# A hybrid attention kernel: the fill of the causal layer moved behind the value products, with a rate for each key tile, and V's staging tile chosen by layer

## The chip, the cores and the metric

One core of one Trainium2 chip runs the kernel; the other seven are idle. The metric is the device time of one execution in microseconds (us). The engines are PE (TensorE: matmuls into PSUM banks), PEld (its weight loads), DVE (VectorE), ACT (ScalarE), POOL (GpSimd) and SP (SyncE, which here only issues DMAs). Each works through its own queue in order, and they wait for each other by semaphores.

## The reference

Sixteen sequences of 512 tokens and 256 channels pass through four attention layers, each with 16 heads of 16 channels: a causal one ("a"), one with two token groups ("f"), a rotary one ("b"), and "f" again with the same weights.

```python
x = x + attn_a(layernorm(x))     # causal
x = x + ffn(layernorm(x))        # attention within two groups of tokens
x = x + attn_b(layernorm(x))     # rotary
x = x + ffn(layernorm(x))

def attn_a(x):
    Q, K, V = x @ Wq.T + bq, x @ Wk.T + bk, x @ Wv.T + bv
    ...
    scores = einsum('bhqd,bhkd->bhqk', Qh, Kh) / sqrt(16)
    scores = where(idxs[None, :] <= idxs[:, None], scores, -10000.0)
    out = einsum('bhqk,bhkd->bqhd', softmax(scores), Vh)
    return out.reshape(b, seq, 256) @ Wo.T + bo

def ffn(x):
    q, k, v = split(x @ W_qkv)
    sim = (cosine of each head of q with a fixed direction).mean(-1)
    pos = (sim - sim.min()) / (sim.max() - sim.min()) > 0.9
    # tokens of pos attend to each other and 5 register tokens, the others likewise
    ...
    return out @ W_proj + b_proj
```

The minimum and maximum of `sim` run over all tokens of all sequences, so an "f" layer's attention can only begin when every sequence has been prepared for it.

## The kernel before

The attention runs over quads: four heads of one sequence in one layer, 4 quads a sequence, 64 a layer. The causal layer is layer 0, with quads 0 to 63. A sequence is called an image in what follows.

**Score products.** For every quad PE makes the scores twice. `maxima` makes them with queries as rows (L610, tile s); DVE takes each row's maximum (in the causal layer with L626, which adds the mask on the way and writes mx after a short read of its accumulator). The maxima go through a small DMA (L654, L657) into additional rows of Q, so that the second product (`products.score`, L687, tile t, keys as rows) comes with the maximum already taken away. In the causal layer two mask products follow each of them (L698). ACT takes the exponential of t into a tile e (L702), and `weigh` multiplies e by V (L713, tile po, four heads side by side, eight matmuls as each is done in two passes), summing over the key tiles. After the last key tile ACT copies po away (L729).

**Key tiles.** A quad has NT = 4 key tiles t of 128 keys, and each has two passes p (two heads each, e = 0, 1). In the causal layer the products of key tile t need only the queries from 128 t on: t is 512, 384, 256 and 128 wide for t = 0, 1, 2, 3. I call t = 0 and 1 wide and t = 2 and 3 narrow. In a narrow tile the two passes share the halves of the same two PSUM tiles. The maxima run AHEAD = 20 steps before the products, so that beside the products of t = 0, 1, 2, 3 stand maxima of 384, 512, 128 and 256 columns. All tiles of PE but po come from one pool, `ps_x`, of seven banks.

**Order.** PE's order is that in which the program issues its work (`manual_schedule` for PE); the order of the other engines is made by a scheduler. For each quad and key tile the main loop (L1108 on) issues a step of the maxima, the score for p = 0, the fill, another step of the maxima, the score for p = 1, and then the value products of the key tile before (`waiting`).

**Fill.** All other work comes as generators in the list `fill`, in order of rank: the preparation of an image for a layer (`prep`: layer norm, transposes L340, V products L467, Q and K products L360, and for "f" the similarity L410 to L434), the share of the masked keys (`masked`, L852 to L856), the tail of an image (`tail`: division, turning back L903, projection L922), and the turning of the maxima (L649). Every generator yields a delay or a condition, and the planned ns of its next step: 1362 for a Q or K product, 1380 for a V product or a projection of two tiles, 450 for transposes, 1750 for the similarity. A planner's clock (`clock["now"]`) decides when a delay is over; it also plans three banks for the fill.

`fill_in` adds RATE[layer] to a credit (2100 ns for layer 0), keeps at most twice that, and calls `drain`, which takes the first step that is able until there is none, or until a step costs more than twice the credit left. Besides, `drain(until=...)` makes fill without credit where something is needed now: before the third quad of an image the image before must be divided, and a quad's Q and K must be prepared before they are loaded.

In layer 0 the fill holds the preparation of image b + 2 for layer 0, that of an earlier image for layer 1, `masked`, and the tail of image b - 1. At the end of the layer all that is left is drained, and `split` makes the groups of layer 1.

**Buffers that matter.** Q and K parts are written into tiles of tag `parts` from pool p4 (two buffers): ACT writes the high part (L398 with bias in layer 0, L401 for "f"), DVE the rest (L399, L402), for Q of "f" GpSimd does both (L380, L381). `send` then issues four DMAs on SP for each (L370, L374) to DRAM, from where `load_quad` (L577, on POOL's queue) fetches whole quads, four ahead. A parts buffer is free when its four DMAs have landed. V is put together in one of two staging tiles `vst`, by b % 2 (L478 by DVE in layer 0, L480 by ACT for the others), and stored by L482 on SP; `load_values` (L583) fetches it back.

Of the kernel before, what the change touches and what calls it, by code (L numbers as in the profile page):

```python
# [119 lines left out]
def hybrid_kernel(ctx: ExitStack, tc: tile.TileContext, a: dict, out: bass.AP):  # L120
# [24 lines left out]
    def small(name, dtype=F32):  # L145
        return ps_x.tile([P, S], dtype, tag="x", name=name)
# [84 lines left out]
    vst = []  # L231
    for i in range(2):
        t = res.tile([P, NT, VW], F32, tag=f"vst{i}", name=f"vst{i}")
# [3 lines left out]
    for i in range(2):  # L237
        t = res.tile([P, RW], FR, tag=f"rst{i}", name=f"rst{i}")
# [61 lines left out]
    def prep(layer, b, x):  # L300
# [154 lines left out]

        def values(u):

            v = vst[b % 2]
            xh, xl = st["xh"], st["xl"]
            ps = small(f"pv{n}_{u}")  # L460
            for k in range(2):
                t = 2 * u + k
                ts = slice(t * P, (t + 1) * P)
                seq = [(xl, wh), (xh, wl), (xh, wh)]
                for q, (xx, ww) in enumerate(seq):
                    for c in range(2):
                        nc.tensor.matmul(  # L467
                            ps[:, k * C : (k + 1) * C],
                            xx[:, c, ts],
                            ww[:, c, WV, :],  # L470
                            start=(q == 0 and c == 0),
                            stop=(q == 2 and c == 1),
                        )
            vo = v[:, 2 * u : 2 * u + 2, 0 : H * HV].rearrange("p t (h e) -> p t h e", e=HV)[:, :, :, 0:D]
            vi = ps.rearrange("p (t h d) -> p t h d", t=2, d=D)
            if kind == "a":
                bias = bv.rearrange("p (h d) -> p h d", d=D).unsqueeze(1).to_broadcast([P, 2, H, D])
                nc.vector.tensor_tensor(vo, vi, bias, ALU.add)  # L478
            else:
                nc.scalar.copy(vo, vi)  # L480
            if u == 1:
                nc.sync.dma_start(vd[b], v)  # L482
# [18 lines left out]
        for u in range(2):  # L501
            yield lag, 1380
            values(u)
            lag = 0
# [69 lines left out]
    def load_quad(i):  # L574
        layer, b, g = quads[i]
        for t, d in ((Qs[i % NB], qd[b]), (Ks[i % NB], kd[b])):
            nc.gpsimd.dma_start(t, d[:, :, 2 * g : 2 * g + 2, :].rearrange("e r h s -> (e r) h s"))  # L577
# [3 lines left out]
    def load_values(layer, b):  # L581
        t = p2.tile([P, NT, VW], F32, tag="v", name=f"v{layer}_{b}")
        nc.sync.dma_start(t, vd[b])  # L583
        V[layer, b] = t
# [406 lines left out]
    def push(gen, rank):  # L991

        k = sum(s.rank <= rank for s in fill)
        fill.insert(k, Steps(gen, rank))

    def push_tail(layer, b):
        push(tail(layer, b), 1)

    def push_call(f, after=None):
        def gen():  # L1000
            yield (lambda: busy["prep"] == 0 and (not after or after in tailed)), 0
            f()

        push(gen(), 1)

    def drain(credit=None, until=None):

        while fill and not (until and until()):
            now = clock["now"]
            able = [s for s in fill if s.ready <= now and (s.next == 0 or banks[0] <= now) and s.open()]  # L1010
            if not able:
                if credit is not None:
                    return
                clock["now"] = min(max(s.ready, banks[0] if s.next else 0) for s in fill if s.open())
                continue
            s = able[0]
            if credit is not None:
                if s.next > 2 * max(0, credit["ns"]):
                    return
                credit["ns"] -= s.next  # L1020
            s.run()

    RATE = {0: 2100, 1: 1350, 2: 1250, 3: 700}
    credit = {"ns": 0}

    def fill_in(layer):

        credit["ns"] = min(credit["ns"] + RATE[layer], 2 * RATE[layer])
        drain(credit)

    def load_through(i):
        while loaded["n"] <= min(i, len(quads) - 1):
            j = loaded["n"]
            layer, b, g = quads[j]
            if (layer, b) not in prepared:
                drain(until=lambda: (layer, b) in prepared)
            if j >= NB:
                l_, b_, g_ = quads[j - NB]
                if PLAN[l_] == "f":
                    drain(until=lambda: (l_, b_, g_ // 2) in registered)  # L1040
            load_quad(j)
            loaded["n"] += 1

    def prep0(b, x=None):
        push(prep(0, b, load_x(0, b) if x is None else x), 2)
        busy["first"] += 1
        constant_rows(b)
# [8 lines left out]
    def advance(to, budget=0):  # L1056

        while taken["n"] < to:
            n = taken["n"]
            load_through(n // (2 * NT))  # L1060
            k, r = divmod(n, 2 * NT)
            if r == 0:
                taken["steps"], taken["end"] = maxima(k)
            taken["steps"][r]()
            clock["now"] += 230
            taken["n"] += 1
            if r == 2 * NT - 1:
                push(taken["end"](), 0)
            if budget:
                at = clock["now"]  # L1070
                drain({"ns": budget})
                clock["now"] = max(clock["now"], at + budget)

    waiting = None
    for i, (layer, b, g) in enumerate(quads):
        kind = PLAN[layer]
        alone = b == 0 and g == 0 and (layer == 0 or kind == "f")
        held = kind != "f" and layer + 1 < len(PLAN) and PLAN[layer + 1] == "f"
        end = (layer + 1) * B * NG if held else len(quads)
        if b or g or layer:  # L1080
            load_through(min(end - 1, i + 4))
        if g == 0:
            load_values(layer, b)
            if kind == "f":
                first, second = registers(layer, b)
                push(first, 2)
                push(second, 2)
        if layer == 0 and g == (1 if b == 0 else 0):
            if b == 0:
                push_call(late_constants)  # L1090
            if b + 2 < B:
                prep0(b + 2)
        if g == 2 and i > NG:
            before = (layer, b - 1) if b else (layer - 1, B - 1)
            drain(until=lambda: before in divided)
        if kind == "a" and g == 1:
            push(masked(b), 2)
        if b == 0 and g == NG - 1 and layer + 1 < len(PLAN):
            push_call(lambda layer=layer: W.__setitem__(layer + 1, load_weights(layer + 1, False)))
        if b == 0 and g == NG - 2:  # L1100
            push_call(lambda layer=layer: WP.__setitem__(layer, load_weights(layer, True)), layer and (layer - 1, B - 1))
        if alone:
            advance((2 * NT) * i + AHEAD, 900)
        if i not in put:
            drain(until=lambda: i in put)
        score, weigh = products(i)
        for t in range(NT):
            for p in range(2):  # L1108
                advance(min(2 * (NT * i + t) + p + 1 + AHEAD, 2 * NT * end))
                score(t, p)  # L1110
                clock["now"] += 230 + TURN
                if p == 0:
                    fill_in(layer)
                elif waiting:
                    waiting()
                    clock["now"] += 868 + TURN
                    waiting = None
            if t == 0 and g == 0 and (b > 0 or (layer > 0 and kind != "f")):
                push_tail(*((layer, b - 1) if b else (layer - 1, B - 1)))
            if i == 0:  # L1120
                load_through(i + 4) if t == NT - 1 else None
            waiting = lambda weigh=weigh, t=t: weigh(t)
        if kind != "f" and b == B - 1 and g == NG - 1 and layer + 1 < len(PLAN):
            waiting()
            waiting = None
            push_tail(layer, b)
            drain()
            split(layer + 1)
# [46 lines left out]
```

## Time and profile before

| what | us |
|---|---|
| runs, median of 3 | 4260.31 (4257.6 to 4260.97) |
| profiled execution | 4242.52 |
| its span, first to last instruction | 4240.7 |
| PE busy | 3937.4 (93%) |
| DVE busy | 3207.0 (76%) |
| ACT busy | 2631.8 (62%) |
| POOL busy | 1820.8 (43%) |
| last mask product of the causal layer ends | 1270.9 |
| mean granted clock of PE | 0.946 |

A time in the text is from the start of the span unless it is a length. In the profile, `out<-in` names tiles, `L610` is a line of the kernel, and what follows an arrow in brackets is the idle time of that engine and what ended it. PE's matmuls are pipelined and their ends are modelled, so their starts tell more than their lengths. The granted clock is the share of PE's full clock.

### The profile page before, as it was taken

The page shows a single profiled execution, that of the slowest core. Times are in us where ns is not written, and L with a number is a line of the kernel's source. Part 1 is how long each engine was busy: PE and PEld are TensorE (multiplying, and loading weights), DVE is VectorE, ACT ScalarE, POOL GpSimd, SP SyncE. Part 2 cuts the span into 40 slices and gives each one's busy share as a digit, 9 for nine tenths or more (in the row PEclk, how much of TensorE's full clock was granted, in tenths as well). Part 3 has the DMA queues.
Part 4 walks back from the last instruction along what each step waited for, and adds up shares of the span by engine and source line. Part 5 has one row for each costly group of instructions (what it writes and reads, how often), then busy time and mean ns, then how long its engine had stood idle before and what let it go on. Part 6 is the DMA issues. An engine that isn't in the chain of part 4 may idle for free.

```text
span 4240.7 us, 79626 instructions
## 1 busy us (share of the span) xinstructions
PE 3937.4 (93%) x27440; PEld 2051.1 (48%) x27440; DVE 3207.0 (76%) x7488; ACT 2631.8 (62%) x5288; POOL 1820.8 (43%) x2421
## 2 busy tenths in 40 slices
PE   3899999999995999999999999999999599999999
PEld 2565656565553444444444444444444334444444
DVE  4676776667654888888888788888886389999996
ACT  1444454444452777777777667777777267777777
POOL 2124545354543256656665634444444412222221
PEclk6899999899996999999999999999999689999999
DMA  9556566666645345555554645455554623333331
GB/s 300 160 159 187 182 200 181 189 184 190 193 128 167 96 137 170 163 149 165 171 162 152 186 146 169 146 167 168 164 157 126 188 85 114 122 116 114 119 121 51
DMA packets 294722, 661.84 MB, mean 156 GB/s; under 512 B 51624, under 2 KB 90032, under 8 KB 294320
## 3 DMA queue, kind: packets, MB, share of 16 engines
q1 hardware_dynamic: 204080, 384.02, 28.9%
q0 software_dynamic: 90240, 272.73, 21.6%
q8 instruction: 219, 3.59, 0.3%
q14 instruction: 183, 1.50, 0.1%
HBM read 379.46 MB, written 298.06 MB: 160 GB/s over the span
## 4 chain that ended last, share of the span: by engine, by line
PE 72%; DVE 10%; DMA 7%; SPq 3%; ACT 3%; issue 3%; POOL 2%; ACTq 0%; DVEq 0%; POOLq 0%
PE po L713 19%; PE s L610 15%; PE t L687 11%; DVE mx L619 5%; PE pv L467 5%; PE pj L922 4%; PE pq L360 4%; DMA qd<-tq 3%; PE pk L360 3%; PE ot L884 2%; POOL nd L432 2%; DVE sc L626 1%; PE rs L759 1%; PE t L698 1%; SPq L568 1%
## 5 line engine op out<-in xcount | busy, mean ns | idle before, releaser
L702 ACT ACTIVATE e<-t 128x512 f32<-128x512 f32 (+2 forms) x3840 | 2017.6, 588 | 824.2 <-PE t L687 538.6
L619 DVE TENSOR_REDUCE mx<-s 128x1 f32<-128x512 f32 x3072 | 1944.4, 681 | 334.7 <-PE s L610 326.2
L610 PE MATMUL s<-ks,qs 52*128 52x512 f32 (+4 forms) x4096 | 1030.8, 481 | 92.3 <-DMA ks<-kd 78.1
L687 PE MATMUL t<-qs,ks 52*128 52x512 f32 (+4 forms) x4096 | 1000.2, 402 | 103.5 <-ACT e L702 35.5
L713 PE MATMUL po<-e,v 128*32 128x512 f32 (+1 forms) x8192 | 1031.1, 576 | 5.1 <-ACT o L729 3.9
L610 PEld LDWEIGHTS s<-ks,qs 48*128 48x128 f32 (+1 forms) x4096 | 429.9, 191 | 1085.7 <-ACT e L702 310.9
L687 PEld LDWEIGHTS t<-qs,ks 50*128 50x128 f32 (+1 forms) x4096 | 496.8, 191 | 302.3 <-DVE mx L619 102.6
L626 DVE CUSTOM_DVE_ANT_0 sc<-s,mask_s_bf 128x128 bf16<-128x128 f32 (+3 forms) x1024 | 497.7, 486 | 160.5 <-PE s L610 78.6
L577 POOL DMA_DIRECT2D qs<-qd x256 | 153.6, 601 | 811.5 <-PE t L687 530.7
L657 POOL DMA_DIRECT2D qs<-md x512 | 268.5, 529 | 543.7 <-DMA md<-ms 516.2
L432 POOL TENSOR_TENSOR nd<-nd,nhalf 128x16 f32<-128x16 f32 x120 | 346.1, 2902 | 22.5 <-DVE nd L423 22.5
L713 PEld LDWEIGHTS po<-e,v 128*32 128x32 f32 x8192 | 162.6, 109 | 271.9 <-issue 194.3
L309 POOL TENSOR_SCALAR xn<-x,nm,st 128x256 f32<-128x256 f32 x256 | 141.4, 557 | 117.7 <-PE xp L340 111.1
L698 PE MATMUL t<-mask_t_bf 64*128 64x128 bf16 x2048 | 189.4, 234 | 0.0
L380 POOL CAST tq<-yq 128x512 fp32r<-128x512 f32 x80 | 49.1, 613 | 267.9 <-DMA qd<-tq 92.5
L884 PE MATMUL ot<-ident,o 128*128 128x128 f32 x1024 | 148.2, 288 | 16.3 <-DVE tq L399 7.1
L577 POOL DMA_DIRECT2D ks<-kd x256 | 140.1, 548 | 52.1 <-issue 14.5
L729 ACT COPY o<-po 128x512 f32<-128x512 f32 x256 | 153.3, 599 | 7.4 <-PE po L713 7.0
L884 PEld LDWEIGHTS ot<-ident,o 128*128 128x128 f32 x1024 | 117.1, 146 | 47.8 <-DVE mx L619 10.1
L340 PE MATMUL xp<-ident,xn 128*128 128x128 f32 x512 | 89.1, 299 | 46.0 <-POOL xn L309 43.7
L930 DVE TENSOR_TENSOR x<-pj,x 128x512 f32<-128x512 f32 x128 | 87.1, 680 | 55.0 <-PE pj L922 50.5
L347 ACT CAST xh<-xp 128x512 fp32r<-128x512 f32 x128 | 76.0, 595 | 84.1 <-PE xp L340 83.9
(358 smaller groups left out, 4991.6 us busy)
## 6 DMA issues: line engine op xcount, KB each, us to landing
qs<-qd POOLq DMA_DIRECT2D x256, 512.0 KB, 4.5
ks<-kd POOLq DMA_DIRECT2D x256, 512.0 KB, 5.3
qd<-tq SPq DMA_DIRECT2D x256, 256.0 KB
kd<-tk SPq DMA_DIRECT2D x256, 256.0 KB
vd<-vst SPq DMA_DIRECT2D x64, 576.0 KB
v<-vd SPq DMA_DIRECT2D x64, 576.0 KB
qd<-tq SPq DMA_DIRECT2D x256, 128.0 KB
kd<-tk SPq DMA_DIRECT2D x256, 128.0 KB
```

The source lines that it names most:

```text
L360: nc.tensor.matmul(dst, ww[:, c, w, cols], xx[:, c, :], start=(k == 0 and c == 0), stop=(k == 2 and c == 1))
L432: nc.gpsimd.tensor_tensor(nd[:, 0, t], nd[:, 0, t], nhalf[:, t], ALU.pow)
L577: nc.gpsimd.dma_start(t, d[:, :, 2 * g : 2 * g + 2, :].rearrange("e r h s -> (e r) h s"))
L610: nc.tensor.matmul(st["ps"][e][:, (p % m) * end :][:, :end], q[r, p, t * P : (t + 1) * P], k[r, p, :end], start=True, stop=True,)
L619: nc.vector.tensor_reduce(st["mx"][:, e, p, t : t + 1], st["ps"][e], AX.X, ALU.max, negate=True)
L626: nc.vector.tensor_tensor_reduce(w, st["ps"][e][:, (i % m) * end :][:, :end], late["mask_s"][:, S - end :], 1.0, -3.0e38, ALU.add, ALU.max ...
L657: nc.gpsimd.dma_start(q[r : r + 2], d[:, e].rearrange("k j t p -> k j (t p)"))
L687: nc.tensor.matmul(ps[e], k[rows[e], p, t * P : (t + 1) * P], q[rows[e], p, q0:], start=True, stop=(kind != "a"),)
L698: nc.tensor.matmul(ps[e][:, :P], mk[:, 0], mk[:, 1], start=False, stop=(o == 1))
L702: st["exp", t] = nc.scalar.activation(e_[:, : m * w], st["ps"][e][:, : m * w], AF.Exp)
L713: mm = nc.tensor.matmul(st["po"][32 * j : 32 * j + 32, q0:], v[:, t, h * HV : h * HV + 32], E.pop((t, j)), start=(t == 0), stop=(t == NT - 1),
L884: nc.tensor.transpose(ps[:, g * P : (g + 1) * P], O[layer, b, g][:, t * P : (t + 1) * P], ident)
```

## The change

```diff
@@ values
-            v = vst[b % 2]
+            v = vst[layer % 2]
...
-    RATE = {0: 2100, 1: 1350, 2: 1250, 3: 700}
+    RATE = {0: (1400, 1400, 2800, 2800), 1: 4 * (1350,), 2: 4 * (1250,), 3: 4 * (700,)}
     credit = {"ns": 0}

-    def fill_in(layer):
+    def fill_in(layer, t):

-        credit["ns"] = min(credit["ns"] + RATE[layer], 2 * RATE[layer])
+        credit["ns"] = min(credit["ns"], RATE[layer][t]) + RATE[layer][t]
         drain(credit)
...
                 score(t, p)
                 clock["now"] += 230 + TURN
-                if p == 0:
-                    fill_in(layer)
-                elif waiting:
+                if p == 0 and layer:
+                    fill_in(layer, t)
+                if p == 1 and waiting:
                     waiting()
                     clock["now"] += 868 + TURN
                     waiting = None
...
             if i == 0:
                 load_through(i + 4) if t == NT - 1 else None
+            if not layer:
+                fill_in(layer, t)
             waiting = lambda weigh=weigh, t=t: weigh(t)
```

In layer 0 the fill of a key tile is issued after both passes of its scores and after the value products of the key tile before, and no longer between the two passes. The credit of layer 0 now depends on the key tile: 1400 ns at t = 0 and 1, 2800 ns at t = 2 and 3; what is carried over is cut to the rate of the tile it is carried into. In layers 1 to 3 place and rate of the fill stay. The tail of the image before, which is put on the list at the first key tile of a new image, is now listed before that tile's fill. V's staging tile is chosen by the layer: all images of layers 0 and 2 use the one, those of layers 1 and 3 the other.

## The prediction

> **What bounds it now.** The causal layer alone is changed, so I read the page first for where that layer lies.
>
> ```profile
> span 4240.7 us, 79626 instructions
> ...
> PE   3899999999995999999999999999999599999999
> ...
> PEclk6899999899996999999999999999999689999999
> ```
>
> The mask products (L698), which only this layer has, end at 1271 us: slices 1 to 11 of 106 us each. PE is at nine tenths there, yet the granted clock falls in it and hardly at all in the layers behind. Next the windows of the steady part and of two short stretches in it (columns: window, its length, busy time and count of PE, weight loads, DVE, ACT, POOL, then granted clock, DMA share, GB/s):
>
> ```profile
> 150.00:1230.00 1080.00, 1012.94 (x8284) 642.74 (x8281) 740.20 (x2750) 519.11 (x1095) 489.41 (x583) 0.93 0.60 181
> ...
> 782.00:788.00 6.00, 5.50 (x37) 3.47 (x38) 3.57 (x15) 2.93 (x7) 6.00 (x3) 0.50 0.56 138
> ```
>
> PE idles 1080 - 1013 = 67 us, and the clock is granted at either full or half (782 to 788 us), so 0.93 means 2 x 0.07 x 1080 = 151 us at half clock. A fit over the 59 quads of this stretch (duration against counts of each kind of fill matmul, idle time and half-clock time, 0.4 us left over) gives 1.06 us for a us of idle and 0.34 us for a us of half clock. So stalls cost 67 + 51 = 118 us here, and the rest is PE work that the change leaves as it is: a quad takes 18.4 us on average. Then who stops PE, and who stops ACT (us in total, times, longest):
>
> ```profile
> PE t L687 <- ACT e L702: 24.9, 12, 5.7
> PE t L687 <- DVE tk L402: 7.2, 5, 1.9
> PE ot L884 <- DVE tq L399: 7.1, 4, 2.2
> ...
> PE t L687 <- DVE mx L626: 3.8, 8, 1.7
> PE t L687 <- DVE tk L399: 2.4, 2, 1.4
> ```
> ```profile
> ACT tk L401 <- DMA qd<-tq: 44.7, 13, 7.0
> ACT tk L398 <- DMA qd<-tq: 35.0, 18, 5.1
> ```
>
> The score products wait for exponentials, and ACT stands before a copy of K or Q into one of two send buffers (pool p4), whose last DMA has not landed; DVE's half of the copy stands with it. One such case in the timeline (start, length; PE, then ACT):
>
> ```profile
> 549.55 0.62 PE L360 MATMUL pk<-xh,whq 128*128 128x512 f32 x2
> ...
> 553.05 0.85 PE L713 MATMUL po<-e,v 128*32 128x384 f32 x8
> 553.83 0.39 PE L610 MATMUL s<-ks,qs 48*128 48x256 f32 x2
> 554.07 0.32 PE L687 MATMUL t<-qs,ks 50*128 50x128 f32 x1
> 558.52 0.47 PE L687 MATMUL t<-qs,ks 50*128 50x128 f32 x1 [4.13 <-ACT e L702]
> ```
> ```profile
> 557.39 0.59 ACT L401 CAST tk<-pk 128x512 fp32r<-128x512 f32 x1 [5.51 <-DMA qd<-tq]
> 557.87 1.09 ACT L702 ACTIVATE e<-t 128x512 f32<-128x512 f32 x2
> ```
>
> ACT stands from 551.9 to 557.4; PE goes on until all seven PSUM banks of ps_x are held, and stops at the second tile of t=3, whose exponentials come behind the copy. Last, ACT and DVE in the wide and the narrow tiles, by shape (busy us, mean ns, idle):
>
> ```profile
> L702 ACT ACTIVATE e<-t 128x512 f32<-128x512 f32 x354 | 192.2, 596 | 145.3 <-PE t L698 144.5
> L626 DVE CUSTOM_DVE_ANT_0 sc<-s,mask_s_bf 128x512 bf16<-128x512 f32 x232 | 159.3, 687 | 33.6 <-PE s L610 14.2
> L626 DVE DVE_READ_ACCUMULATOR2_ANT mx<- 128x1 f32 x939 | 77.6, 83 | 0.0
> ```
>
> **The change, part by part.** It adds and removes no instruction of the tensor work. I write F(t) for the fill in the round of key tile t.
>
> *The place of the fill.* Before, a round is [t, F, s, t, po]; after, [s, t, s, t, po, F]. What counts is how much PE can do once a copy in F has stopped ACT and DVE: it ends when seven banks are held, one by the copy's own product. For t=2 and 3 both pairs of heads share a tile (two banks for s, two for t). Before, F stands inside them: four banks held, one for the copy, two for the next s, and PE has left s, t, masks, po and the next s. With spacings from the timeline (two s 0.17 to 0.43 us by width, two t 0.17 to 0.45, four masks 0.2, eight po 0.21 to 0.85) that is 1.3 us for F(2) and F(3), 1.9 for F(1), 1.6 for F(0). After, F(1) and F(2) are followed by a whole narrow round in four banks, its po, and two steps of the next fill of 1.42 us each (pk, 548.52 to 549.9): 4.3 to 4.5 us. F(3) and F(0) are followed by a wide round in which s, t, s take six banks: 1.3 to 1.4 us. So the half of the fill that stands in F(1) and F(2) gains some 2.8 us of cover, the other half loses 0.2. The order on ACT and DVE isn't written out, so the copies may stand elsewhere in it; hence both ends.
>
> The waits that this bears on are 24.9 + 7.2 + 2.4 = 34.5 us. None gone gives 0; all gone gives -34.5, and with their part of the half clock, 34.5/67 x 51 = 26, -60. I take half of both, as half of the fill is covered: -17 and -13, **-30 us**.
>
> *How far the clock follows.* Half-clock spells begin behind waits as short as 1.2 to 2.2 us in this trace (2.15 us at 653 us, half clock from 655.7), so I let the clock follow the idle time. The Trainium skill, "TensorE: Matmul & The Clock Gate", section "HAM oscillation — how this bites in real kernels", has as its abstract rule that only gaps of more than about 3.4 us matter. By it, only the four waits over 3.4 us would count, the clock's share of the gain would mostly fall away, and the sum would be some -9 instead of -22. The trace's short waits speak against it here.
>
> *The wide rounds.* In a round of t=0 or 1 eight tiles come with no fill and no po between, so the last t needs the first s reduced: 0.55 to 0.69 us plus 0.08 for the read, behind DVE's copy of the fill's last product (0.75). Before, po (0.21 or 0.85 us) stood among these eight. Nothing in the trace shows this order. Lower end: 0, if DVE keeps up. Upper end: the whole po time missed in both wide rounds and a little less, 0.8 us a quad x 64 = +51. Nearest is today's row for it, t waiting for mx, 3.8 us in 59 quads; with less room I take three times that, **+8 us** more.
>
> *The rates.* A quad's credit stays 4 x 2100 = 1400 + 1400 + 2800 + 2800 = 8400 ns. With steps of 1362 the pattern goes from 2, 1, 2, 1 to 1, 1, 2, 2. A wide round with one step is level on three engines: t=0 has 4 x 0.596 + 0.595 for o + 0.69 for a copy = 3.7 us on ACT, 3.6 on PE (2.13 + 1.42); t=1 has 4 x 0.77 + 0.75 = 3.8 on DVE, 4.2 on PE. PE leads or is level everywhere, so I cost this at **0**; without a step in a wide round the cover is gone, and ACT's 2.98 or DVE's 3.08 stand against 2.13 or 2.77 of PE: 0.3 to 0.85 us lost in each. Unused credit carried into a wide round is now cut to 1400 (2100 before), so late fill catches up more slowly; today one forced drain each 12 quads (quad 17, 29, 41, 53 take 29 to 30 us) costs about 2.2 of idle and 10 us of half clock, 5.6 us: from -22 (all four go) to +56 (ten more), taken as 0.
>
> *V's staging.* One buffer for a layer adds a wait of the V copies (DVE L478, ACT L480) for the last store of the same layer (L482). In the trace such copies lie at least 43 us behind that store's issue, and the page's DMA rows land loads of like size in 4.5 to 5.3 us: **0**. Without that cover the copy would hold DVE's maxima behind it for about 5 us an image.
>
> *Queues.* A fill step's sends (four issues on SP, 0.6 us each) move with it, by less than a round. F(3) now ends a quad, so its GpSimd work (xn 0.56, pow 2.9 us) is ahead of the next load_quad on that queue; the load serves the quad four later, 73 us on. The tail's x load and GpSimd addition come one round earlier. All 0.
>
> **Sum:** -30 + 8 = -22 us. Against the profiled execution (4242.5 us, 1.8 of it around the span) that is 4220; the runs' median, 4260.3, stands 17.8 above it, so **4238 us**.
>
> **The rivals.**
> - *Relief and new waits cancel.* The wide rounds cost 26 rather than 8: -30 + 26, **4256 us**. For it: ACT and DVE have as little room in wide rounds as shown. Against: mx waits are rare today.
> - *Slower: the send buffers.* Two steps in each of F(2) and F(3) put four copies within two rounds, one per 2.2 us instead of 3.1, while a buffer comes free 7 us after its fill (GpSimd finishes a tq at 550.4 in the case above, ACT gets its buffer at 557.4), one per 3.5. The fourth copy is late by 3 x (3.5 - 2.2) = 3.9 us, against 1.2 before: 2.7 more, in F(3), where only 1.3 are covered: 1.4 us in each of 32 preparations, +45, and with a half-clock spell of 7 us (x 0.34) in half of them +38. With -30 - 4: **4309 us**. It decides once copies wait over about 3 us in F(3). For it: ACT's 80 us of such waits. Against: the steps are seldom all ready together.
> - *Fill comes late.* Half of the 128 wide rounds find no step (0.58 us each, +37), and +8: with -30, **4275 us**. For it: the cut credit. Against: the credit is 8400 for about 7340 of planned work.
>
> **How the numbers follow.** Forecast 0.50, cancelling 0.14, send buffers 0.20, late fill 0.16. The forecast's own range is 4190 to 4252. About 0.2% (8.5 us) is what a measurement tells from no change, so faster 0.50, same 0.14, slower 0.36. The range must hold most of the last two: 4180 to 4325; below it lie the whole 60 us and vanished drains, above it both slower mechanisms at once.
>
> **What would show it.** Right: t waiting for e or tk falls from 34.5 to about 17 us in the causal layer, the clock there from 0.93 to about 0.95, its last mask product comes near 1249 us, and the later layers keep their lengths. Wrong: ACT's waits of tk or tq for DMA growing beyond 80 us, t waiting for mx far above 12 us, more quads of 29 us, or a wait at L478 or L480. A change in the layers behind would make the whole argument wrong.

## The result, and the profile after

The changed kernel takes 4305.55 us (median of 4 runs, 4292.49 to 4311.03), the kernel before 4258.95 in the same comparison: 1.0112 times as long, 95% interval 1.0079 to 1.0144. It is slower by 47 us, where a gain of 22 was forecast. The page of the profiled execution (4310.3 us):

```profile
span 4308.3 us, 79671 instructions
...
PE   3898999999995999999999999999999599999999
...
PEclk6789999889897799999999989999999789999999
```

The instructions are the same in number on every computing engine. In slices 1 to 11 of the causal layer (counted from 0, as in the prediction) the clock's digit is under 9 five times, against twice before. The windows from the first to the last mask product, first of the kernel before, then of the changed one (columns as in the prediction):

```profile
100.90:1270.90 1170.00, 1091.06 (x8882) 689.00 (x8882) 777.69 (x2876) 558.36 (x1180) 516.10 (x613) 0.92 0.59 177
```
```profile
99.30:1316.90 1217.60, 1129.24 (x8882) 707.01 (x8885) 792.33 (x2876) 555.37 (x1180) 509.13 (x610) 0.89 0.57 169
```

The layer is 47.6 us longer. PE's idle time in it is 88.4 us against 78.9, and by the clock records 262 us against 180 are at half clock. Another 19 us of the difference between the two spans lie behind `split`, where place and rate of the fill are the old ones (2919 us before, 2938 after); the seven variants below that keep two send buffers and the whole computation take 2922 to 2939 us there, so I count this as spread between executions. The profiled execution of the kernel before is also quicker than most of its executions, 4242.5 us against a median of 4259. What PE waited for in the changed kernel, in the stretch of the prediction (150 to 1230 us):

```profile
PE t L687 <- ACT e L702: 21.2, 15, 3.1
PE t L687 <- DVE mx L626: 12.8, 46, 1.4
PE s L610 <- DVE tk L399: 8.6, 4, 3.8
PE s L610 <- ACT e L702: 7.6, 7, 1.5
PE s L610 <- DVE tk L402: 4.9, 1, 4.9
PE t L687 <- DVE tk L402: 4.3, 1, 4.3
```

PE's waits for exponentials (e) and for copies of K and Q (tk, tq) haven't shrunk, over the whole layer 49 us before and 56 after; a good part has moved from t to s. ACT's copies, in the same stretch:

```profile
ACT tk L398 <- DMA qd<-tq: 54.9, 14, 6.7
ACT tk L401 <- DMA qd<-tq: 23.0, 6, 5.3
ACT tk L401 <- DMA vd<-vst: 17.6, 2, 9.0
ACT tq L398 <- DMA kd<-tk: 5.7, 2, 5.3
ACT tq L398 <- DMA qd<-tq: 4.3, 1, 4.3
```

That is 105 us, against 91 before. One such case in the timeline, PE and then ACT:

```profile
415.71 0.62 PE L360 MATMUL pk<-xh,whq 128*128 128x512 f32 x2
...
417.70 0.66 PE L340 MATMUL xp<-ident,xn 128*128 128x128 f32 x4
...
418.82 0.71 PE L687 MATMUL t<-qs,ks 50*128 50x512 f32 x2
...
424.57 0.69 PE L610 MATMUL s<-ks,qs 48*128 48x384 f32 x1 [4.90 <-DVE tk L402]
```
```profile
423.21 0.58 ACT L401 CAST tk<-pk 128x512 fp32r<-128x512 f32 x1 [5.26 <-DMA qd<-tq]
```

The copy stands in F(2). PE gets through the narrow round behind it and two small steps of F(3) (xp and st), then into the wide round of the next quad, and stops, out of banks, 3.3 us after the product. ACT stands until 423.2 and PE loses 4.9 us.

### The profile page after: what moved, and what is told of

Same layout as the page of the kernel before. It is cut to its first block, busy times and chain, and to the rows that moved or that the text cites. A ratio compares the mean times of both kernels' runs of the same rounds, so it can differ in the third digit from the quotient of the medians.

```text
span 4308.3 us, 79671 instructions
## 1 busy us (share of the span) xinstructions
PE 3988.8 (93%) x27440; PEld 2074.4 (48%) x27440; DVE 3222.0 (75%) x7488; ACT 2628.1 (61%) x5288; POOL 1815.2 (42%) x2421
## 4 chain that ended last, share of the span: by engine, by line
PE 55%; DVE 7%; ACT 2%; SPq 2%; DMA 2%; issue 1%; POOL 1%; ACTq 0%; POOLq 0%; DVEq 0%
PE po L713 16%; PE s L610 12%; PE t L687 9%; DVE mx L619 5%; PE pj L922 3%; PE pv L467 3%; PE pq L360 2%; PE pk L360 2%; PE ot L884 2%; PE rs L759 1%; SPq L568 1%; ACT e L702 1%; PE pa L903 1%; POOL nd L432 1%; PE mt L649 1%
## 5 line engine op out<-in xcount | busy, mean ns | idle before, releaser
L610 PE MATMUL s<-ks,qs 52*128 52x512 f32 (+4 forms) x4096 | 1047.3, 483 | 117.7 <-DMA ks<-kd 81.3
L687 PE MATMUL t<-qs,ks 52*128 52x512 f32 (+4 forms) x4096 | 1023.2, 408 | 109.4 <-ACT e L702 35.8
L713 PE MATMUL po<-e,v 128*32 128x512 f32 (+1 forms) x8192 | 1052.1, 587 | 4.6 <-ACT e L702 3.4
L610 PEld LDWEIGHTS s<-ks,qs 48*128 48x128 f32 (+1 forms) x4096 | 443.7, 194 | 1017.6 <-ACT e L702 300.0
L698 PE MATMUL t<-mask_t_bf 64*128 64x128 bf16 x2048 | 198.6, 237 | 0.0
L402 DVE TENSOR_TENSOR tk<-pk,tk 128x512 fp32r<-128x512 f32 x64 | 44.1, 689 | 132.0 <-ACT tk L401 122.2
```

What stands on the lines that cost most here:

```text
L610: nc.tensor.matmul(st["ps"][e][:, (p % m) * end :][:, :end], q[r, p, t * P : (t + 1) * P], k[r, p, :end], start=True, stop=True,)
L687: nc.tensor.matmul(ps[e], k[rows[e], p, t * P : (t + 1) * P], q[rows[e], p, q0:], start=True, stop=(kind != "a"),)
L698: nc.tensor.matmul(ps[e][:, :P], mk[:, 0], mk[:, 1], start=False, stop=(o == 1))
L713: mm = nc.tensor.matmul(st["po"][32 * j : 32 * j + 32, q0:], v[:, t, h * HV : h * HV + 32], E.pop((t, j)), start=(t == 0), stop=(t == NT - 1),
```

## The experiments

Each was timed in five rounds beside the kernel before on one chip; the ratio is to that kernel. The other columns are in us, for the causal layer, from one profiled execution each: the length from first to last mask product, PE's idle time in it, time at half clock, and the rest, length - 1.06 x idle - 0.38 x half clock (fits over the quads of five of these kernels give 0.86 to 1.08 and 0.33 to 0.42 for the two factors). One execution is a small sample: before and e3_staging issue PE's work of this layer in the same order and are equally fast, and yet differ by 14 us in length and 42 in time at half clock.

| run | what | ratio (95%) | length | idle | half | rest |
|---|---|---|---|---|---|---|
| before | | 1 | 1170 | 79 | 180 | 1018 |
| after | the change | 1.0112 (1.0079 to 1.0144) | 1218 | 88 | 262 | 1024 |
| e1_place | place, even rate | 0.9949 (0.9929 to 0.9969) | 1145 | 66 | 149 | 1018 |
| e2_rates | rates, old place | 1.0072 (1.0052 to 1.0092) | 1208 | 89 | 235 | 1024 |
| e3_staging | staging alone | 0.9997 (0.9978 to 1.0016) | 1184 | 77 | 222 | 1018 |
| e6_wide | place, rates turned round | 1.0144 (1.0124 to 1.0164) | 1227 | 115 | 253 | 1010 |
| e7_cap | change, carry as before | 1.0030 (1.0015 to 1.0046) | 1181 | 76 | 209 | 1021 |
| e16_after_one | change, one copy a fill | 1.0069 (1.0049 to 1.0089) | 1190 | 104 | 189 | 1007 |
| e17_place_one | even rate, one copy a fill | 1.0029 (1.0014 to 1.0044) | 1182 | 88 | 199 | 1014 |
| e5_before_send3 | before, 3 send buffers | 0.9852 (0.9833 to 0.9871) | 1140 | 54 | 160 | 1022 |
| e4_send3 | change, 3 send buffers | 0.9858 (0.9837 to 0.9878) | 1137 | 61 | 141 | 1020 |
| e12_cap_send3 | change, carry, 3 buffers | 0.9856 (0.9833 to 0.9878) | 1140 | 64 | 151 | 1015 |
| e9_place_send3 | even rate, 3 buffers | 0.9753 (0.9735 to 0.9771) | 1092 | 40 | 98 | 1012 |
| e22_before_send4 | before, 4 buffers | 0.9799 (0.9776 to 0.9823) | 1116 | 49 | 123 | 1017 |
| e20_after_send4 | change, 4 buffers | 0.9725 (0.9710 to 0.9740) | 1094 | 44 | 85 | 1016 |
| e21_place_send4 | even rate, 4 buffers | 0.9716 (0.9699 to 0.9733) | 1081 | 36 | 82 | 1012 |
| e13_after_fixed | change, sends from a fixed tile | 1.0048 (1.0031 to 1.0064) | 1245 | 156 | 273 | 975 |
| e15_before_fixed | before, sends from a fixed tile | 1.0090 (1.0074 to 1.0107) | 1255 | 173 | 261 | 973 |

### The parts of the change

```diff
 # e1_place: after, with
-    RATE = {0: (1400, 1400, 2800, 2800), ...
+    RATE = {0: 4 * (2100,), ...
 # e2_rates: after, with
-                if p == 0 and layer:
+                if p == 0:
                     fill_in(layer, t)
...
-            if not layer:
-                fill_in(layer, t)
 # e3_staging: before, with
-            v = vst[b % 2]
+            v = vst[layer % 2]
 # e6_wide: after, with
-    RATE = {0: (1400, 1400, 2800, 2800), ...
+    RATE = {0: (2800, 2800, 1400, 1400), ...
```

> The changed kernel with the old rate, 2100 at every key tile: the new place of the fill and V's staging alone. Theory of the place (with neither fill nor value products inside a wide round, eight score tiles crowd seven banks, PE waits for DVE's maxima, and works so thinly there that the clock falls): most of the loss stays, ratio to the kernel before 1.007 to 1.014, and the waits of t for mx stay near 13 us. Theory of the rates (two steps in each narrow round bring Q and K copies too close for two send buffers): the loss goes, 0.997 to 1.003.

> The kernel before with the new rates and V's staging by layer; the fill stays between the two passes. Theory of the place: no loss, 0.995 to 1.004. Theory of the rates: the loss is here, 1.007 to 1.014, with ACT's waits of tk and tq for DMA well over the 91 us of before.

> The kernel before with V's staging tile by layer alone. Both theories: no difference, 0.997 to 1.003. If the staging makes V copies wait for the last store, some of the 1.011 shows here, with waits of L478 or L480 for a DMA.

> The changed kernel with the rates turned round: 2800 at the wide key tiles, 1400 at the narrow. Theory of the place: the wide rounds are short of fill, so more of it there lengthens them and PE no longer waits for DVE; less loss than the change, 1.000 to 1.008. Theory of the rates: the copies are as close together as in the change, only elsewhere, and now ahead of wide rounds with little cover: 1.010 to 1.020.

Staging costs nothing. The new place alone, with staging, is **faster** by 0.51%, and the uneven rates alone slower by 0.72%; at the new place they cost 1.0112 - 0.9949 = 1.6%. Turned round they cost more still, so more fill in the wide rounds doesn't mend it, though e6_wide also has twice as many quads over 27 us as the kernel before (eight against four). PE's and ACT's waits in e1_place, same stretch:

```profile
PE t L687 <- DVE mx L626: 12.1, 48, 0.6
PE pk L360 <- ACT e L702: 10.5, 3, 3.7
PE s L610 <- DVE tk L402: 10.0, 5, 2.3
...
PE t L687 <- ACT e L702: 2.9, 2, 2.7
```
```profile
ACT tk L401 <- DMA qd<-tq: 22.0, 8, 3.6
ACT tk L398 <- DMA qd<-tq: 21.8, 4, 6.7
ACT tk L401 <- DMA md<-ms: 14.3, 4, 5.6
ACT tk L401 <- DMA v<-vd: 3.5, 1, 3.5
```

The copies wait 62 us for DMAs, against 91 before and 105 in the change. Waits of t for mx are as long as in the change: they belong to the place, and not to the rates. e2_rates did not have the longer ACT waits that were expected of it (99 us against 98 before, over the whole layer), so at the old place this reading of the rates' cost isn't confirmed.

### Buffers and carry

Three buffers need room: four small tiles of `split` and of the similarity go into shared buffers (shown shortened).

```diff
 # e4_send3: after; e5_before_send3: before; e9_place_send3: e1_place; each with
-        pool("p4", 2),
+        pool("p4", 3),
...
-        fl = p1.tile([P, 4, n], F32, tag="fl", name=f"fl{layer}")
+        fl = ptmp.tile([P, 4, n], F32, tag="tmp", name=f"fl{layer}")
...
 # e7_cap: after; e12_cap_send3: e4_send3; each with
-        credit["ns"] = min(credit["ns"], RATE[layer][t]) + RATE[layer][t]
+        credit["ns"] = min(credit["ns"] + RATE[layer][t], sum(RATE[layer]) // 2)
```

> The changed kernel with three send buffers for Q and K parts (room made by putting four small tiles of the similarity and of split into shared buffers). Theory of the send buffers (uneven rates bring the copies too close): ACT's waits of tk and tq for DMA nearly vanish and the loss goes, ratio to the kernel before 0.985 to 1.000. Theory of late fill (uneven rates with a carry cut to the next tile's rate leave steps undone, and forced drains make quads of 25 to 30 us): most of the loss stays, 1.004 to 1.012, and the long quads stay.

> The kernel before with three send buffers: what the buffers are worth without the change. Theory of the send buffers: the waits of before for DMA (some 100 us on ACT in the causal layer) go with 10 to 40 us of the time, 0.990 to 0.998, a smaller gain than in the changed kernel. Theory of late fill: the same gain here as in the changed kernel.

> The changed kernel with its uneven rates, but the credit kept up to 4200 ns at every key tile, as before. Theory of late fill by the carry: the drains go and with them most of the loss, 0.994 to 1.003. Theory of the send buffers: as many copies as close together, 1.007 to 1.014.

> The new place of the fill with the old even rate 2100 and three send buffers, the version that could beat both. Theory of the send buffers: the two gains add up, 0.985 to 0.993. Theory of late fill: the drains are gone already with the even rate, and the buffers add little, 0.991 to 0.996.

> The changed kernel, uneven rates, with both mends: three send buffers and the credit kept up to 4200 ns at every key tile. Place with an even rate and three buffers gave 0.9753, uneven rates with three buffers 0.9858. Theory of the copies (uneven rates cost by the waits of Q and K copies, through bunching that carry and buffers both ease): between the two, nearer the better, 0.975 to 0.981. Theory of the wide rounds (with little fill in them ACT and DVE set the pace there): the unevenness is still there, 0.983 to 0.988.

With three buffers the change is level with the kernel before (0.9858 and 0.9852), and the even rate at the new place beats both at **0.9753**, some 104 us. Old order and even rate gain more from the third buffer than was expected of them (0.9852 against 0.990 at best, 0.9753 against 0.985). The rates' cost goes from 1.6% to 1.05% only, and e12_cap_send3 lies in the range of the wide rounds' theory, so that one still stood here. The carry takes half of the cost away with two buffers (1.0030, the upper end of what late fill had named) and nothing with three, so late fill is no cause by itself; the work that the program's planner had to force out of turn in quads 4 to 62 is smaller in the change (21 us as planned) than before (37). Nor does the cost go by how long ACT's copies wait: e7_cap has lost half of it, with 118 us of such waits in the layer against 119 in the change.

### Copies that wait for nothing

The first try took the wait away by letting every send read a fixed tile, a copy of the first x, so that Q and K of all images are left out. Its twin with the even rate gave no result.

```diff
 # e13_after_fixed: after; e15_before_fixed: before; each with
+    fixed = res.tile([P, 2, S], FR, tag="fixed", name="fixed")
...
-                    t[r].bitcast(F32),
+                    fixed[r].bitcast(F32),
...
-    t[r, 0, :].bitcast(F32)
+    fixed[r, 0, :].bitcast(F32)
```

> The changed kernel, but all sends of Q and K parts read a fixed tile (a copy of the first x) in place of the copy just made: Q and K of every image are left out, traffic and number of instructions stay, and no copy waits for a DMA. Theory of the copies: with the waits gone the loss of the uneven rates goes, so this is within 0.3% of the next run. Theory of the wide rounds: it stays some 0.8 to 1.1% slower than the next.

> The kernel before with sends from a fixed tile, Q and K left out: what the place alone is worth without any wait of a copy for a DMA. If the place pays only by covering such waits (as the prediction has it), this is within 0.3% of the even rate at the new place; if it also pays otherwise, 0.5 to 1% slower than that.

Both came out slower. PE's longest wait in e13_after_fixed:

```profile
PE t L689 <- DMA qs<-md: 102.5, 6, 38.0
PE t L689 <- DVE mx L628: 7.4, 31, 0.4
PE t L689 <- ACT e L704: 4.3, 4, 3.6
```

No copy waits for a DMA, and the wait for e falls to 4.3 us, but sends that depend on nothing go out at other times: SP stands before some of them (L372) until older loads have read the same DRAM, 77 us in 13 waits, and the maxima's DMA is issued on the same queue. A new wait of 102 us took the place of the old. The two settle nothing about the rates.

The second try limits copies to one in each fill of the causal layer.

```diff
 # e16_after_one: after; e17_place_one: e1_place; each with
-        drain(credit)
+        drain(credit, one=not layer)
...
+            if one and copied:
+                able = [s for s in able if s.next != 1362]
+                if not able:
+                    return
             s = able[0]
+            copied = copied or s.next == 1362
```

> The changed kernel with one more rule for the fill of the causal layer: at most one Q or K product step (and so one copy into a send buffer) in each key tile's fill; rates uneven as in the change, two send buffers. Theory of the copies (uneven rates put two or three copies into one fill, they wait for their buffers' DMAs and hold exponentials and maxima behind them): most of the loss goes, 0.990 to 1.000, and PE's waits for e and tk fall from about 48 us to under 25. Theory of a cost of the uneven fill in itself: 1.006 to 1.013.

> The new place with the even rate 2100 and the same rule, two send buffers. Theory of the copies: few fills held two copies here, so little changes, 0.988 to 0.996, and e16_after_one comes within 0.4% of it. Theory of a cost of the uneven fill: e16_after_one stays 0.8% or more behind.

Both ranges of the theory of the copies were missed: 1.0069, which is what a cost of the uneven fill in itself had named, and 1.0029. The distance of the two, 0.4%, is what the copies had named, but mostly because the even rate became slower. ACT's waits of copies do fall, to 55 and 37 us (150 to 1230 us), but the delayed steps run into another wait, here in e16_after_one:

```profile
PE xp L340 <- POOL xn L309: 29.1, 5, 6.9
PE t L687 <- ACT e L702: 20.1, 13, 3.1
```

So the runs with one copy in a fill don't show that two in one fill are the point.

The third try gives four buffers. The tables of the rotary layer make the room: its angles are left out, both factors are 1; the causal layer is untouched by that.

```diff
 # e20_after_send4: e4_send3; e21_place_send4: e9_place_send3; e22_before_send4: e5_before_send3; each with
-        pool("p4", 3),
+        pool("p4", 4),
...
-            cos, sin = late["cos"], late["sin"]
+            cos = sin = ones.unsqueeze(1).to_broadcast([P, NT, P])
```

> The changed kernel with four send buffers; the two tables of the rotary layer make room (its angles are left out: both factors are 1). Three buffers left uneven rates 1.05% behind even ones. Theory of the copies: with four the distance to e21_place_send4 shrinks to 0.7% or less. Theory of a cost of the uneven fill: it stays at 0.9% or more.

> The new place with the even rate and four send buffers, angles left out as well. Both theories: a little faster than with three, 0.968 to 0.976; it is here for the distance to the run before it.

> The kernel before with four send buffers, angles of the rotary layer left out as in the two runs with four: what the place alone is worth once no copy waits for a DMA (new place with even rate: 0.9716). If the place pays by covering stops of ACT and DVE, as the prediction had it, nothing is left: 0.970 to 0.974. If it also pays otherwise: 0.976 to 0.982.

Now the uneven rates cost 0.9725 - 0.9716 = 0.1%, less than the two intervals resolve. In the causal layer alone the uneven rates are longer by 73 us with two buffers, 46 with three and 13 with four, and the last is no more than two executions of one order differ by (before and e3_staging, 14). All that ACT's copies wait for DMAs in e20_after_send4 between 100 and 1180 us, and then in e21_place_send4:

```profile
ACT tk L396 <- DMA qd<-tq: 3.0, 3, 1.2
ACT tq L396 <- DMA vd<-vst: 1.1, 1, 1.1
ACT tq L396 <- DMA kd<-tk: 0.7, 1, 0.7
```
```profile
ACT tk L399 <- DMA kd<-tk: 0.8, 1, 0.8
```

And the windows of the causal layer of e20_after_send4, e21_place_send4 and e22_before_send4:

```profile
96.30:1190.40 1094.10, 1050.46 (x8881) 667.41 (x8885) 785.53 (x2877) 561.07 (x1180) 513.76 (x612) 0.96 0.62 189
```
```profile
97.00:1178.20 1081.20, 1045.07 (x8886) 665.57 (x8889) 787.61 (x2878) 560.78 (x1182) 509.31 (x611) 0.96 0.63 191
```
```profile
96.00:1211.80 1115.80, 1066.57 (x8882) 676.48 (x8885) 783.81 (x2878) 562.96 (x1181) 509.86 (x611) 0.95 0.61 186
```

The clock is at 0.96 in the first two, against 0.89 in the change. The place, on the other hand, still pays with four buffers: 0.9716 against 0.9799, and the layer is 35 us shorter than in e22_before_send4, with 13 us less idle time and 40 us less at half clock.

## Why the prediction was wrong, point by point

**The place of the fill** was forecast at -30 + 8 = -22 us. With staging alone beside it, it measures -0.51% of 4260, some -22 us. Its parts agree less well than the sum. The waits named in the forecast, of t for e and tk, fall from 34.5 to 3 us and not to 17, but others come up at s and pk: all of PE's waits for e, tk and tq in the layer fall from 49 to 26 us. The waits of t for mx rise from 3.8 to 12.1 us (8 more forecast). Time at half clock goes from 180 to 149 us, worth 31 x 0.38 = 12 us (13 forecast), but e3_staging, with the old place, has 222, so one execution each doesn't fix that term. And the reason given was too narrow: that the place pays by covering stops behind copies fits the waits with two buffers, but with four such stops are nearly gone in both kernels and it still pays 0.8%. There xn, the maxima's DMA and copies of x hold PE less, and the half-clock time is 40 us less; which part of the new order does that isn't shown. That the sum fits so well is luck in part.

**The rates: "PE leads or is level everywhere, so I cost this at 0."** This step failed. At the new place uneven rates cost 1.6%, about 70 us, which turns the gain of the place into the loss of the whole. In the profiles (after against e1_place) it is 73 us of the layer: 22 us more idle time and 113 us more at half clock, by the factors of the table 24 and 43 us. What was right in it is the sum over engines: the rest in the table, what is left when stalls and half clock are taken off, stays between 1007 and 1024 us in every kernel whose computation is whole in the causal layer. The step went by engine loads of an average round and did not ask what the rates do to waits. Its pattern of steps wasn't the real one either: counted in PE's order over quads 4 to 62, forced ones with them, 38, 18, 20 and 31 Q and K products stand in the fills of t = 0, 1, 2 and 3 before, and 18, 8, 32 and 50 in the change.

**The rival of the send buffers** (4309 us, chance 0.20) comes nearest to what happened. Its place was right: copies stand for the DMAs of a send buffer, and in the case shown the stop ends in a wide round. At the new place the cost of the rates goes as buffers are added: 1.6% with two, 1.05% with three, 0.1% with four, while ACT's copies wait 119, 47 and 5 us for DMAs in the layer with uneven rates and 67, 19 and 1 with even ones. So there the cost needs the shortage of send buffers. Its detail, two copies in each narrow fill, is not confirmed. The narrow fills do hold 82 Q and K products in quads 4 to 62, against 50 in e1_place, and 27 of them hold two or more, against 11; but e7_cap is nearly the same in this (76, and 24) at half the cost, and the runs with one copy a fill did not mend it. Which pattern of steps turns the shortage into lost time, and why uneven rates cost 0.7% at the old place without longer waits of copies, is open.

**Late fill** (4275 us, 0.16) is not the cause by itself: forced work is no more than before, four quads take over 25 us in each of the two kernels, and the carry, worth half of the rates' cost with two buffers, is worth nothing with three.

**The cover of F(2)** was put at 4.3 us, with two fill steps of 1.42 behind the narrow round. In the case at 415.7 us it was 3.3, as F(3) had only two short transposing steps. A cover made of fill is only there when steps are ready.

**V's staging and the queues**, costed at 0, hold: e3_staging is at 0.9997. The two waits for V's store (17.6 us) in the changed kernel are put down to K copies, whose sends share SP's queue with that store.

**The clock.** The Trainium skill ("TensorE: Matmul & The Clock Gate", section "HAM oscillation — how this bites in real kernels") has the rule "no PE-idle gaps >~3.4µs", which the prediction took to mean that shorter gaps do no harm. These runs speak against that again: from 149 us on, three waits of PE in the changed kernel's causal layer are over 3.4 us (4.9, 4.3 and 3.8), but there are 28 half-clock spells, 230 us in all.

## What to carry to other kernels

A copy that waits for a send buffer holds up everything behind it on its engine until that buffer's DMAs have landed (ACT stood 5.3 us in the case at 415.7 us). So count a buffer's whole turn, here some 7 us, against the rate at which copies can come, before the order of the work around them is tuned. A schedule that is level in engine time may still lose time by where its waits fall. Try the parts of a change apart: here one of them gained 0.5%, and with a third buffer, which alone gives 1.5%, the two together give 2.5%.

## What the runs showed of the hardware

PE falls to half clock also where its records hardly show idle time. Of 28 half-clock spells in the changed kernel's causal layer (from 149 us on), 8 have less than 0.5 us of PE idle time in the 7 us ahead of them; in e21_place_send4 it is 1 of 9. One of these in two windows of the changed kernel:

```profile
809.00:819.00 10.00, 9.41 (x94) 6.04 (x95) 9.74 (x40) 5.23 (x12) 8.40 (x3) 1.00 0.76 240
819.00:829.00 10.00, 10.00 (x49) 7.03 (x47) 5.61 (x19) 4.53 (x11) 6.68 (x10) 0.50 0.35 107
```

PE counts as busy for 9.4 of 10 us at full clock, most of the rest being idle time at the start, and then falls to half for 10 us, with half as many matmuls. The stretch ahead holds narrow score products, many 128-column transposes (ot, xp) and one wide round, and DVE is busy for 9.7 of its 10 us. So a PE that looks busy in the 7 us ahead, by records whose ends are modelled, may still lose its clock; what the clock follows is not shown.
